# Gating a feed-forward layer in token halves, handed out one pair of slices later

## The chip, the cores and the metric

The kernel is one program on one core of a Trainium2 chip. The metric is the device time of one execution in microseconds (us); lower is better. Everything is 32-bit floating point.

## What is computed

Eight sequences of 128 tokens with 512 features go through one cross-attention layer and one gated feed-forward layer. The reference, cut to its frame and to the part that the change touches:

```python
x = x + xattn(layernorm(x), ctx, mask, position_bias, ...)      # 32 heads of 128
# feed-forward: Wg, Wu are (1376, 512), Wd is (512, 1376)
h    = layernorm(x)
gate = einsum('bsh,ih->bsi', h, Wg) * ag
up   = einsum('bsh,ih->bsi', h, Wu) * au
out  = einsum('bsi,hi->bsh', silu(gate) * up, Wd) * ad
x    = x + out
```

`silu(g)` is `g * sigmoid(g)`. The step `silu(gate) * up` is called the gating below.

## The kernel before

The kernel runs in stages: keys, values and queries; attention by groups of four heads; the output projection; and the feed-forward layer, which takes the last fifth of the time. Only the last stage matters here.

All 1024 tokens lie along the free dimension, in two halves of 512[...]. The 1376 inner features are cut into ten slices of 128 and one of 96. The slice of 96 is worked out apart (`last_slice`). The ten others go in five pairs, `i` from 0 to 4. In each pair a Strassen-like scheme (`seven`) replaces eight block products by seven, for the gate weights (`t = 0`) and the up weights (`t = 1`) in turn: fourteen products, counted by `n` from 0 to 13. A product is two `nc.tensor.matmul` calls (L688), which the profile shows as four MATMULs. After each product its PSUM bank is added into or copied to two tiles in SBUF. For `n` = 0 and 1 that is a copy on ScalarE (L235), for 2 and 3 an addition on VectorE (L240), for 4 to 9 copies on ScalarE (L245), and for 10 to 13 additions on VectorE (L251). The gate's result goes to the tiles `gate[0]` and `gate[1]`, one for each slice of the pair; the up result goes straight to `act[2*i]` and `act[2*i+1]`.

The banks tie TensorE to the other engines. Products 4 to 9 use the two banks of products 2 and 3 again, so product 4 cannot start until the addition of product 2 (L240) has read its bank. In the same way 12 and 13 reuse the banks of 10 and 11. Each pair takes fresh banks for products 0, 2 and 10 from a ring of seven.

After the fourteenth product of a pair, `gated` is called for each of its two slices. It issues a sigmoid on ScalarE (L639) into a tile `sg`, then `sg = gate * ag * sg` (L640) and `act = act * au * sg` (L643) on VectorE, each over all 1024 tokens. VectorE runs its queue in order, so what is queued there first delays what follows.

GpSimd (POOL) forms the weight sums for the coming pairs (`sums_a`, L193 to L196: four additions for the gate weights, four for the up weights). The sums of pair `i + 2` go into buffers that pair `i` gives back with its last products, so they run just as pair `i` ends. The weights themselves are loaded by the SP queue (L617).

`gate`, `sg`, and several tiles that live to the end of the stage come from one pool, `acts`, of 18 equal buffers: four of `x1`, four of `h2`, four of token sums `T1` to `T4`, and the rest for `gate` and `sg`. When all pairs are done, the loop over `b` multiplies with the down weights: eleven products for each sequence (L712, `ic` 10 first and then 0 to 9), a scaling and the residual addition on VectorE (L716, L717), and the store (L718).

The instructions stand in the engines' queues in the order that a scheduling step gives them. It follows the program where it can, but lets an instruction that is ready go ahead of one that is not.

Of the kernel before, what the change touches and what calls it, by code (L numbers as in the profile page):

```python
# [2 lines left out]

# [13 lines left out]
P = 128  # L17
# [8 lines left out]
def xattn_ffn_kernel(  # L26
# [164 lines left out]
    def sums_a(eng, a11, a12, a21, a22, s1, s2, s4):  # L191

        eng.tensor_tensor(s1, a21, a22, ADD)  # L193
        eng.tensor_tensor(s2, s1, a11, SUB)
        eng.tensor_tensor(a21, a11, a21, SUB)
        eng.tensor_tensor(s4, a12, s2, SUB)  # L196
        return {1: a11, 2: a12, 3: s4, 4: a22, 5: s1, 6: s2, 7: a21}
# [26 lines left out]
    def seven(name, tiles, product, part, pool, tag="mm"):  # L224


        def bank(i):
            return [
                pool.tile([P, 512], F32, tag=tag, name=f"mm_{name}_{i}_{t}") for t in tiles
            ]  # L230

        m = bank(2)
        for t in tiles:
            product(2, t, m[t], True)
            nc.scalar.copy(part(1, 1, t), m[t])  # L235
            yield
        m = bank(1)
        for t in tiles:
            product(1, t, m[t], True)
            nc.vector.tensor_tensor(part(1, 1, t), part(1, 1, t), m[t], ADD)  # L240
            yield
        for i, r, c in ((6, 1, 2), (7, 2, 2), (4, 2, 1)):
            for t in tiles:
                product(i, t, m[t], False)
                nc.scalar.copy(part(r, c, t), m[t])  # L245
                yield
        m = bank(5)
        for i, r, c in ((5, 2, 2), (3, 1, 2)):
            for t in tiles:
                product(i, t, m[t], i == 5)  # L250
                nc.vector.tensor_tensor(part(r, c, t), part(r, c, t), m[t], ADD)  # L251
                yield
# [359 lines left out]
    def load_gate_up(i, eng=nc.sync):  # L612
        c0, n = i * 2 * P, min(2 * P, INTER - i * 2 * P)
        tiles = []
        for nm, src in (("wg", wgT), ("wu", wuT)):
            t = fw.tile([P, DC, 2 * P], F32, tag="w", name=f"{nm}_{i}")
            eng.dma_start(  # L617
                t[:, :, :n], src[:, c0 : c0 + n].rearrange("(c p) n -> p c n", p=P)
            )
            tiles.append(t)  # L620
        return tiles

    def load_down():
        t = wdp.tile([P, NI, D], F32, tag="wd", name="wd")
        full = INTER // P
        nc.sync.dma_start(t[:, :full, :], wdT[: full * P, :].rearrange("(c p) n -> p c n", p=P))
        if INTER % P:
            nc.sync.dma_start(t[: INTER % P, full, :], wdT[full * P :, :])
        return t

    act = [actp.tile([P, T], F32, tag="act", name=f"act_{ic}") for ic in range(NI)]
# [5 lines left out]
    def gated(act, gate, up, ic, m, sg):  # L637

        nc.scalar.activation(sg, gate, AF.Sigmoid, scale=ag_sb[:m, ic : ic + 1])  # L639
        nc.vector.scalar_tensor_tensor(  # L640
            sg, gate, ag_sb[:m, ic : ic + 1], sg, ALU.mult, ALU.mult
        )
        nc.vector.scalar_tensor_tensor(  # L643
            act, up, au_sb[:m, ic : ic + 1], sg, ALU.mult, ALU.mult
        )

    def last_slice(th):

        ic, m = NI - 1, INTER - (NI - 1) * P
        o = []  # L650
        for w, nm in zip(alone, ("gp", "up")):
            o.append(ps.tile([P, 512], F32, tag="m", name=f"{nm}_{th}"))
            for c in range(DC):
                nc.tensor.matmul(  # L654
                    o[-1][:m], w[:, c, :m], h2[c // HC, th][:, c % HC, :],
                    start=(c == 0), stop=(c == DC - 1),
                )
        sg = work.tile([P, 512], F32, tag="pT", name=f"sg_{th}", bufs=4)
        gated(act[ic][:m, bass.ts(th, 512)], o[0][:m], o[1][:m], ic, m, sg[:m])
# [10 lines left out]
    nc.vector.tensor_tensor(t4, h2[1, 0], t2, SUB)  # L670
    h2_t = {1: h2[0, 0], 2: h2[1, 0], 3: h2[1, 1], 4: t4, 5: t1, 6: t2, 7: t3}

    for i in range(NP):
        ws, gate = [], [acts.tile([P, T], F32, tag="a", name=f"gate_{i}_{r}") for r in range(2)]
        for nm, w in zip("gu", gate_up[i]):
            s = fw.tile([P, 3, HC, P], F32, tag="S", name=f"S_{nm}{i}")
            ws.append(sums_a(
                nc.gpsimd, w[:, :HC, :P], w[:, HC:, :P], w[:, :HC, P:], w[:, HC:, P:],
                s[:, 0], s[:, 1], s[:, 2],
            ))  # L680
        if i + 1 < NP:
            gate_up.append(load_gate_up(i + 1))
        if i == 0:
            wd = load_down()

        def product(n, t, out, first):
            for c in range(HC):
                nc.tensor.matmul(  # L688
                    out, ws[t][n][:, c, :], h2_t[n][:, c, :],
                    start=(first and c == 0), stop=(c == HC - 1), skip_group_check=True,  # L690
                )

        def part(r, c, t):
            return (gate[r - 1], act[2 * i + r - 1])[t][:, bass.ts(c - 1, 512)]

        for n, _ in enumerate(seven(f"f{i}", range(2), product, part, ps, "m")):
            if i == 0 and n == 3:
                last_slice(1)
        for r in range(2):
            ic = 2 * i + r  # L700
            sg = acts.tile([P, T], F32, tag="a", name=f"sg_{ic}")
            gated(act[ic], gate[r], act[ic], ic, P, sg)

    for b in range(B):
        r = work.tile([P, D], F32, tag="aT", name=f"r_{b}")
        parts = 1 if b + 1 < B else 2
        for k in range(parts):
            cols = bass.ts(k, D // parts)
# [53 lines left out]
```

## Time and profile before

| what | value |
|---|---|
| median of 3 runs | 1152.94 us (1151.9 to 1153.74) |
| the profiled execution: its own time | 1155.07 us |
| the profiled execution: span from first to last instruction | 1153.3 us |
| TensorE (PE) busy | 1116.4 us, 97% |
| VectorE (DVE) busy | 501.0 us, 43% |
| ScalarE (ACT) busy | 317.4 us, 28% |
| GpSimd (POOL) busy | 307.3 us, 27% |
| share of the chain that ended last: PE, DVE | 90%, 4% |
| mean granted TensorE clock | 0.992 of full speed |

The span runs from the first instruction to the last; the time of the profiled execution is 1.77 us longer, which lies around it. It is one execution, 2.13 us above the median. "Busy" counts the instructions' own durations; PEld is the loading of weights into TensorE. The chain that ended last is followed back from the last instruction, at each step to what released it; only work on that chain sets the time.

### The profile page before, as it was taken

The page shows a single profiled execution, that of the slowest core. Times are in us where ns is not written, and L with a number is a line of the kernel's source. Part 1 is how long each engine was busy: PE and PEld are TensorE (multiplying, and loading weights), DVE is VectorE, ACT ScalarE, POOL GpSimd, SP SyncE. Part 2 cuts the span into 40 slices and gives each one's busy share as a digit, 9 for nine tenths or more (in the row PEclk, how much of TensorE's full clock was granted, in tenths as well). Part 3 has the DMA queues.
Part 4 walks back from the last instruction along what each step waited for, and adds up shares of the span by engine and source line. Part 5 has one row for each costly group of instructions (what it writes and reads, how often), then busy time and mean ns, then how long its engine had stood idle before and what let it go on. Part 6 is the DMA issues. An engine that isn't in the chain of part 4 may idle for free.

```text
span 1153.3 us, 12296 instructions
## 1 busy us (share of the span) xinstructions
PE 1116.4 (97%) x4286; PEld 729.4 (63%) x4286; DVE 501.0 (43%) x937; ACT 317.4 (28%) x889; POOL 307.3 (27%) x255
## 2 busy tenths in 40 slices
PE   6899999999999999999999999689999999999998
PEld 3564444445867677686858688578888864444445
DVE  4541111116555556555555557724433253433311
ACT  2521112223444344434344433301000022222000
POOL 5331221116333333333223314530000034330000
PEclk9999999999999999999999999899999999999999
DMA  9114423257646465555554446864222322110000
GB/s 281 43 37 149 178 110 110 109 204 252 187 138 200 145 192 162 176 181 174 184 172 148 135 146 199 256 217 170 92 92 80 116 99 73 36 37 1 15 31 28
DMA packets 117534, 154.38 MB, mean 134 GB/s; under 512 B 12033, under 2 KB 71681, under 8 KB 117473
## 3 DMA queue, kind: packets, MB, share of 16 engines
q1 hardware_dynamic: 114784, 149.93, 40.4%
q10 hardware_dynamic: 2192, 2.10, 0.6%
q0 software_dynamic: 496, 1.58, 0.4%
q8 instruction: 34, 0.56, 0.2%
q14 instruction: 28, 0.22, 0.1%
HBM read 101.14 MB, written 52.43 MB: 133 GB/s over the span
## 4 chain that ended last, share of the span: by engine, by line
PE 90%; DVE 4%; DMA 4%; issue 1%; ACT 1%; SPq 0%; ACTq 0%; DVEq 0%
PE mm_q L261 17%; PE mm_v L279 16%; PE mm_k L261 15%; PE m L469 15%; PE mm_f L688 9%; PE dn L712 7%; PE sc L301 4%; PE av L357 4%; DMA turned<-tt 1%; DMA wk<-in_wkT_dram 1%; DVE sg L640 1%; DMA a<-att 1%; DVE act L643 1%; PE tp L152 1%; PE up L654 1%
## 5 line engine op out<-in xcount | busy, mean ns | idle before, releaser
L296 POOL TENSOR_TENSOR s<-pb,mneg 128x512 f32<-128x512 f32 x64 | 81.2, 1269 | 290.7 <-DVE tt L334 234.0
L261 PE MATMUL mm_k<-ctx_sb,wk 128*128 128x512 f32 x256 | 117.4, 603 | 7.5 <-DMA wk<-in_wkT_dram 4.4
L279 PE MATMUL mm_v<-wv,ctx_sb 128*128 128x256 f32 x512 | 115.9, 379 | 1.3 <-DMA wv<-in_wvT_dram 1.3
L261 PE MATMUL mm_q<-hT,wq 128*128 128x512 f32 x256 | 112.5, 592 | 0.0
L469 PE MATMUL m<-wo,a 128*128 128x256 f32 x400 | 100.6, 389 | 9.6 <-DMA a<-att 9.1
L311 ACT ACTIVATE s<-s,nmx 128x128 f32<-128x128 f32 x256 | 99.5, 390 | 37.4 <-DVE nmx L308 37.4
L279 PEld LDWEIGHTS mm_v<-wv,ctx_sb 128*128 128x128 f32 x512 | 95.1, 190 | 14.8 <-DMA wv<-in_wvT_dram 2.1
L362 ACT COPY aT<-av 128x512 f32<-128x512 f32 x64 | 37.5, 586 | 202.9 <-PE av L357 98.5
L261 PE MATMUL mm_k<-ctx_sb,S_k 128*128 128x512 f32 x192 | 87.8, 605 | 4.4 <-DVE k L240 4.0
L469 PEld LDWEIGHTS m<-wo,a 128*128 128x128 f32 x400 | 77.1, 196 | 21.2 <-DMA a<-att 9.5
L261 PEld LDWEIGHTS mm_q<-hT,wq 128*128 128x128 f32 x256 | 48.6, 190 | 60.8 <-issue 60.7
L279 PE MATMUL mm_v<-S_v,ctx_sb 128*128 128x256 f32 x384 | 86.4, 381 | 0.0
L261 PEld LDWEIGHTS mm_k<-ctx_sb,wk 128*128 128x128 f32 x256 | 46.9, 193 | 60.4 <-issue 45.2
L261 PE MATMUL mm_q<-hT,S_q 128*128 128x512 f32 x192 | 85.0, 592 | 0.0
L304 DVE TENSOR_TENSOR s<-sc,s 128x512 f32<-128x512 f32 x64 | 44.2, 690 | 86.0 <-PE sc L301 82.9
L301 PEld LDWEIGHTS sc<-k,q 128*128 128x128 f32 x512 | 67.4, 194 | 17.9 <-issue 13.4
L279 PEld LDWEIGHTS mm_v<-S_v,ctx_sb 128*128 128x128 f32 x384 | 71.7, 190 | 10.6 <-DVE v L251 1.5
L712 PE MATMUL dn<-wd,act 128*128 128x512 f32 (+3 forms) x198 | 75.8, 545 | 0.0
L251 DVE TENSOR_TENSOR q<-q,mm_q 128x512 f32<-128x512 f32 x32 | 22.0, 688 | 114.8 <-PE mm_q L261 114.8
L301 PE MATMUL sc<-k,q 128*128 128x128 f32 x512 | 68.1, 277 | 2.8 <-DMA q<-queries 2.8
L357 PE MATMUL av<-pT,v 128*128 128x128 f32 x512 | 67.9, 277 | 0.0
L261 PEld LDWEIGHTS mm_k<-ctx_sb,S_k 128*128 128x128 f32 x192 | 35.6, 193 | 48.6 <-issue 35.7
(156 smaller groups left out, 1494.3 us busy)
## 6 DMA issues: line engine op xcount, KB each, us to landing
queries<-q SPq DMA_DIRECT2D x32, 512.0 KB, 3.8
q<-queries SPq DMA_DIRECT2D x32, 512.0 KB, 4.5
turned<-tt SPq DMA_DIRECT2D x64, 256.0 KB, 2.2
pT<-turned SPq DMA_DIRECT2D x256, 64.0 KB, 2.5
att<-aT SPq DMA_DIRECT2D x64, 256.0 KB, 2.3
a<-att SPq DMA_DIRECT2D x32, 512.0 KB, 3.4
wq<-in_wqT_dram SPq DMA_DIRECT2D x8, 1024.0 KB, 5.6
wk<-in_wkT_dram SPq DMA_DIRECT2D x7, 1024.0 KB, 6.2
```

Source lines behind the costliest of these rows:

```text
L251: nc.vector.tensor_tensor(part(r, c, t), part(r, c, t), m[t], ADD)
L261: nc.tensor.matmul(out, w[i][:, c, bass.ts(t, P)], src[i][:, c, :], start=(first and c == 0), stop=(c == HC - 1), skip_group_check=True,)
L279: nc.tensor.matmul(out[:, bass.ts(k, HW)], src[i][:, c, bass.ts(2 * t + k, S)], w[i][:, c, :], start=(first and k == 0 and c == 0), stop=( ...
L296: nc.gpsimd.tensor_tensor(s, pb, mneg[:, b : b + 1, :].to_broadcast([P, GH, S]), ALU.add)
L301: nc.tensor.matmul(sc[:, j, :], qT[:, j, bass.ts(b % 2, S)], kT[j][:, cols], start=True, stop=True)
L304: nc.vector.tensor_tensor(s, sc, s, ALU.add)
L311: nc.scalar.activation(s[:, j, :], s[:, j, :], AF.Exp, bias=nmx[:, j : j + 1], accum_out=sm[:, j : j + 1],)
L357: nc.tensor.matmul(av[:, j, :], v[b // 2][:, b % 2, bass.ts(j, P)], pT[:, :, j, :], start=True, stop=True,)
L362: nc.scalar.copy(aT, av)
L469: nc.tensor.matmul(m[n], sa[n][:, c, :], wo_t[g][n][:, c, :], start=(g == order[0] and c == 0 and k % 2 == 0), stop=(g == order[-1] and c ...
L688: nc.tensor.matmul(out, ws[t][n][:, c, :], h2_t[n][:, c, :], start=(first and c == 0), stop=(c == HC - 1), skip_group_check=True,)
L712: nc.tensor.matmul(o, act[ic][:m, bass.ts(b, S)], wd[:m, ic, cols], start=(n == 0), stop=(n == NI - 1),)
```

## The change

The gating is no longer issued whole after the pair. Each slice's gating is cut into two pieces of 512 tokens, and the four pieces of a pair are put on a list. During the next pair's fourteen products one piece is taken from the list after each of the products `n` = 4, 6, 8 and 10, behind that product's own copy or addition. The list is in the order slice 0 first half, slice 0 second half, slice 1 first half, slice 1 second half. So sixteen of the twenty pieces are issued inside a following pair, and the last pair's four after the loop, ahead of the down products. The arithmetic is the same.

```diff
+    gatings = []
     for i in range(NP):
...
         for n, _ in enumerate(seven(f"f{i}", range(2), product, part, ps, "m")):
             if i == 0 and n == 3:
                 last_slice(1)
+            if 4 <= n < 12 and n % 2 == 0 and gatings:
+                gatings.pop(0)()
         for r in range(2):
             ic = 2 * i + r
             sg = acts.tile([P, T], F32, tag="a", name=f"sg_{ic}")
-            gated(act[ic], gate[r], act[ic], ic, P, sg)
+            for cols in (bass.ts(0, 512), bass.ts(1, 512)):
+                gatings.append(partial(
+                    gated, act[ic][:, cols], gate[r][:, cols], act[ic][:, cols], ic, P, sg[:, cols]
+                ))
+    for gating in gatings:
+        gating()
```

More of the change, by code (lines that the diff above doesn't have):

```diff
@@ L2 @@
 from contextlib import ExitStack
+from functools import partial
 import concourse.bass as bass
```

## The prediction

> **What bounds the kernel now.** I read the page's busy shares first, then the feed-forward stage alone (940 us to the end): who waited for whom, the chain that ended last, and the timelines of DVE, ACT and POOL around the end of each pair.
>
> ```profile
> PE 1116.4 (97%) x4286; PEld 729.4 (63%) x4286; DVE 501.0 (43%) x937; ACT 317.4 (28%) x889; POOL 307.3 (27%) x255
> ```
>
> TensorE is busy all but 37 us, so a change in this stage can only win where TensorE stands still. In the stage's list of waits TensorE's matmuls have one entry, three waits for L240, the addition that frees product 2's bank:
>
> ```profile
> PE mm_f L688 <- DVE gate L240: 3.7, 3, 1.2
> ```
>
> The chain that ended last shows the first of them (columns: start us, duration us, what):
>
> ```profile
> 973.40 0.69 DVE act L251
> 974.09 3.29 DVE sg L640 x2
> 977.38 1.19 DVE act L643
> 978.58 0.40 issue
> 978.98 1.31 DVE act L643
> 980.29 0.35 issue
> 980.64 0.69 DVE gate L240
> 981.33 0.14 issue
> 981.46 17.42 PE mm_f L688 x40
> ```
>
> Pair 0's last addition, its four gating instructions and only then L240 of pair 1 stand in DVE's queue. The same nine steps follow at 998.91 and 1024.41. Beside them POOL forms sums, and DVE's gating is slow:
>
> ```profile
> 974.00 3.38 DVE L640 SCALAR_TENSOR_TENSOR sg<-gate,ag_sb,sg 128x1024 f32<-128x1024 f32 x2
> 977.31 3.41 DVE L643 SCALAR_TENSOR_TENSOR act<-act,au_sb,sg 128x1024 f32<-128x1024 f32 x2
> ```
>
> At the fourth end of a pair POOL has nothing left to do. There the two rows of two last 2.47 us each, L240 comes in time and TensorE does not stop. The table by stretch shows it (five stretches of 10 us; the fifth is the last pair's gating under the down products):
>
> ```profile
> 972.00:982.00 10.00, 8.77 (x22) 3.66 (x21) 8.88 (x8) 3.36 (x4) 9.15 (x8) 1.00 0.00 0
> 997.50:1007.50 10.00, 8.77 (x22) 3.66 (x21) 8.89 (x8) 3.36 (x4) 9.15 (x8) 1.00 0.00 0
> 1023.00:1033.00 10.00, 8.77 (x22) 3.67 (x21) 8.89 (x8) 3.36 (x4) 9.15 (x8) 1.00 0.00 0
> 1048.50:1058.50 10.00, 10.00 (x25) 4.48 (x24) 7.13 (x8) 3.37 (x5) 0.00 (x0) 1.00 0.00 0
> 1072.50:1082.50 10.00, 10.00 (x25) 4.49 (x24) 5.88 (x6) 2.19 (x2) 0.00 (x0) 1.00 0.00 0
> ```
>
> The first figure after the length is PE's busy time: 8.77 of 10 at three ends, 10.00 at the fourth. By start times the loss is larger, because the ends of matmuls are modelled: products start 1.715 us apart, but product 4 starts 981.46 - 978.35 = 3.11 us after product 3. That is **1.40 us lost at each of three ends, 4.2 us in all**, the most this change can win by its mechanism.
>
> **What the skill says.** The Trainium skill, "SBUF — State Buffer", section "Who interferes with whom": a VectorE instruction with two SBUF inputs contends with a GpSimd instruction that reads SBUF; one with at most one SBUF input, outside the two-port modes, does not. The trace agrees: L640 and L643 take 1.71 us beside POOL and 1.28 without, POOL's sums 1.71 and 0.73, while L251, with one PSUM input, stays at 0.69. The page calls it an exclusive lock; measured, DVE took 6.64 us from 974.00 to L240 against 4.78 without POOL (1050.52 to 1055.30), and four POOL instructions ran meanwhile, so I use (6.64 - 4.78) / 4 = 0.47 us for each POOL instruction met. "Perfetto Trace Analysis", section "Optimizing Scalar/DVE Operations": "If Scalar/Vector aren't saturated, but are causing bubbles on other engines, breaking up instructions may allow work to be completed sooner." The bubble is there; no run here shows yet whether breaking up helps.
>
> **The change, part by part.** *Halves.* A sigmoid of 128x1024 takes 1142 ns; the nearest row of 128x512 with one per-partition operand is L175, 720 ns (bounds 683, the slice of 96, and 808, L596 with two operands). A half L640 or L643 is nearest to the slice of 96: 748 ns, 529 less than the 1277 of the whole. Queued back to back, whole ones came 4.78 / 4 = 1.195 us apart, so halves come 0.665 apart. Per pair ACT gets 4 x 0.72 - 2 x 1.14 = 0.6 us more and DVE 8 x 0.665 - 4.78 = 0.5 us more. Neither counts: in a pair of 24 us DVE idles 11.9 us ahead of product 10's addition and ACT idles 1.13 us after each copy. What covers them is this idle time; without it the whole would cost 5 x 0.5.
>
> *The move.* If the pieces stay where the program writes them, L240 follows the previous pair's last addition at once. Product 2 ends at 978.35, L240 starts 0.27 later and takes 0.69, and TensorE needs it by 978.35 + 1.715 = 980.06: 0.6 us to spare, all three stalls gone, **-4.2 us**. Later pieces hit idle engines. The tightest is the fourth, behind product 10's addition: that addition ends at 992.98, two halves at 994.31, product 11's addition follows, and TensorE can go on 0.82 us after its start (the distance from L240's start, 980.64, to 981.46) at 995.13; product 13 is due at 995.50. What is queued behind a piece on ACT is the next product's copy, ready 1.715 us after the one before; 0.59 + 0.72 fits.
>
> *Where the queue puts them.* The trace says the queue is not the program's order: `gated` issues L640, L643, L640, L643, yet both L640 run first, since the second was ready when the first L643 was not. A piece's inputs are ready long before product 4. One thing holds it back: in the trace the second slice's sigmoid, whose gate was whole at 969.0 (product 10's addition), did not run before the first's at 972.41, so a tile of `acts` seems not to be begun ahead of one begun earlier in the program. The first piece then has to follow the next pair's first copy (gate tile, 975.12), but needn't wait for product 4. The second piece shares its `sg` tile and follows at once; the third waits for product 6's copy, which begins the next gate tile. So I expect slice 0's two pieces just behind the first copy: sigmoid from 975.7 to 976.4, four halves on DVE from 976.42, done at 979.08 undisturbed, TensorE ready at 979.90, in time. POOL disturbs it: its third and fourth sum of the up weights, 0.69 apart from 974.59, now run at 975.97 and 976.66 and end near 977.4; one or two meet the halves. That adds 0.47 to 0.93: L240 at 979.55 to 980.01, TensorE at 980.37 to 980.83, a stall of 0.31 to 0.77 where 1.40 was. I take 0.4, near one meeting, since two meetings need both sums to be late. **3 x (1.40 - 0.4) = 3.0 us won.** The fourth end keeps 0.16 us to spare.
>
> *The end.* The last pair's eight halves come behind its last addition, 1074.6 + 8 x 0.665 = 1079.9. The first sequence's last down product, the tenth behind 1073.74 at 0.857 each, is due at 1082.3: covered. If it weren't, each 0.1 us late would cost 0.1 us.
>
> *Queues not touched.* No DMA is moved. SP's weight loads wait for products and POOL's sums for products 12 and 13 as before; POOL gets freer. The store queue is the same. Buffers: at the tightest moment `acts` holds 12 lasting tiles, two old gates, two `sg` and two new gates: 18, exactly what there is.
>
> **Sum.** 1155.07 - 3.0 = 1152.1 for the profiled execution. The median before stands 2.13 us lower, so 1152.94 - 3.0 = **1149.9**.
>
> **Rivals.** (1) *The pieces stay behind products 4 to 10:* all 4.2 us won, 1148.7. For it: the program says so. Against it: the reordered L640. 30%. (2) *The bunch ahead of L240 stays long:* all pieces slip ahead, or POOL's lock delays each half as it did each whole; four halves at 0.665 + 0.47 end at 980.96, TensorE at 981.8, 1.7 us late, or 5 us of halves as before. Then 1152 to 1154, no change within noise. Against it: POOL is through by 977.4, and the third piece waits for a gate tile. 15%. (3) *Slower: a nineteenth tile in* `acts`. If one more tile is held when product 6's copy begins the second gate tile, the copy waits until an old gate is given back, in the worst case with the fourth piece: two sigmoids and four halves behind product 6, 985.4 + 1.4 + 2.7 = 989.5, copy and release to 990.2, where product 8 was due at 986.92. That stalls 3.3 us in each of four pairs: 1152.94 + 13.2 - 4.2 = 1162. It decides from 1.05 us a pair. Against it: the count gives 18 and not 19. 5%, and 3% for a slowdown I don't see. My own case has 47%.
>
> **How the numbers follow.** Anything under 1150.6 is faster by over 0.2%, about what a measurement of this kernel can tell from no change. My case spans 3 x 0.63 = 1.9 to 4.2 us won, 1148.7 to 1151.0, and mostly counts as faster; with rival 1 that gives 76% faster. Its slow edge and rival 2 give 16% the same; 8% slower. The range takes in both likely cases, the low edge of rival 2, and the runs' scatter of about 0.8 us: 1148.0 to 1151.9.
>
> **What would show it.** Twice as many L639, L640 and L643 of 128x512 near 720 and 745 ns. In the waits, TensorE's 3.7 us for L240 shrinks below 2 or vanishes; in the stretches around the first three ends PE rises above 9.3. In DVE's timeline four halves stand before L240 (mine) or none (rival 1). The feed-forward stage's POOL sums of the up weights fall from 1.71 us towards 0.73. A wait of ACT's copies on DVE would be rival 3. Three stalls of over 1 us left, or new waits at products 6 to 13, would prove me wrong.

## The result, and the profile after

The changed kernel takes 1151.96 us in the median of 20 runs, against 1153.88 us for the kernel before in the same series. The ratio of the two series is 0.998, with a 95% interval of 0.9974 to 0.9986. That is 2.3 us less (1.6 to 3.0), two thousandths; the two medians by themselves lie 1.9 apart. The prediction forecast 3.0 us less, and so 1149.9 with a range of 1148.0 to 1151.9, from the three runs then shown, whose median was 1152.94. The measured median lies 0.06 above that range, but in the longer series the kernel before is 0.94 higher too: 2.3 us off 1152.94 would be 1150.6. The profiled execution took 1152.01 us, span 1150.2 us, against 1155.07 and 1153.3.

The line of the page with each engine's busy time (share of the span, instructions) shows the added instructions, 20 on DVE and 10 on ACT, and 9.4 us less on POOL, whose sums are lengthened less by VectorE. PE's busy time, which contains modelled ends, differs by several us among the profiles of all kernels here and is not read:

```profile
PE 1120.0 (97%) x4286; PEld 731.4 (64%) x4286; DVE 502.3 (44%) x957; ACT 318.1 (28%) x899; POOL 297.9 (26%) x255
```

In the waits of the feed-forward stage (us in total, times, longest) the one entry of TensorE's matmuls is still there, and smaller. L240 of the kernel before is L241 here:

```profile
PE mm_f L690 <- DVE gate L241: 1.0, 3, 0.3
```

The chain that ended last, at the first end of a pair (start us, duration us, what), answers to the nine steps shown of before:

```profile
974.77 0.02 ACT gate L236
974.80 0.46 issue
975.26 0.73 ACT sg L640
975.99 0.03 issue
976.01 2.13 DVE sg L641 x2
978.14 1.32 DVE act L644 x2
979.47 0.61 DVE gate L241
980.08 0.14 issue
980.22 19.14 PE mm_f L690 x44
```

The gating of slice 0, now four half instructions, still stands ahead of the addition that TensorE needs. It no longer starts at the pair's last addition but behind the next pair's first copy, and it is four halves where four wholes had been. TensorE's rows for products 3 and 4 there:

```profile
978.01 1.88 PE L690 MATMUL mm_f<-h,wu 128*128 128x512 f32 x4
980.22 1.96 PE L690 MATMUL mm_f<-T_h,S_g 128*128 128x512 f32 x4 [0.33 <-DVE gate L241]
```

Product 3 began at 978.01, so product 4 was due 1.715 us later, at 979.73; it began at 980.22. **0.49 us are lost at each of three ends, where it had been 1.40.** The table by stretch (10 us around each end; the first figure after the length is PE's busy time) says the same, with the fourth end again undisturbed:

```profile
971.70:981.70 10.00, 9.67 (x24) 4.09 (x23) 5.68 (x8) 2.30 (x4) 5.74 (x8) 1.00 0.00 0
996.50:1006.50 10.00, 9.67 (x23) 4.10 (x22) 5.43 (x8) 2.29 (x4) 5.54 (x8) 1.00 0.00 0
1021.10:1031.10 10.00, 9.68 (x23) 4.10 (x22) 5.48 (x8) 2.30 (x4) 5.53 (x8) 1.00 0.00 0
1045.50:1055.50 10.00, 10.00 (x25) 4.42 (x24) 5.02 (x8) 2.37 (x5) 0.00 (x0) 1.00 0.00 0
```

Whole-kernel times scatter by several us between runs, and so does the time at which this stage begins. A sharper measure is the stage itself in a profile: from the first matmul of `last_slice` (into `gp`) to the first down product (into `dn`). These rows hold the two times, first of the kernel before, then of the changed one:

```profile
L654 PE MATMUL gp<-h,wg x16: 592/592/592, 934.6 to 952.2; 128*96 128x512 f32 x16
L712 PE MATMUL dn<-wd,act x198: 377/592/594, 1073.7 to 1149.1; 128*128 128x512 f32 x140, 128*128 128x256 f32 x40, 96*128 96x512 f32 x14, 96*128 96x256 f32 x4
L655 PE MATMUL gp<-h,wg x16: 592/592/592, 934.2 to 951.8; 128*96 128x512 f32 x16
L721 PE MATMUL dn<-wd,act x198: 377/592/594, 1070.7 to 1146.1; 128*128 128x512 f32 x140, 128*128 128x256 f32 x40, 96*128 96x512 f32 x14, 96*128 96x256 f32 x4
```

With the two decimals of the timelines that is 1073.74 - 934.55 = 139.19 us before and 1070.68 - 934.21 = 136.47 after. The stage is 2.7 us shorter, which is the three stalls, 3 x (1.40 - 0.49) = 2.7.

### The profile page after: what moved, and what is told of

The parts are those of the page before. It is cut to its first block, busy times and chain, and to the rows that moved or that the text cites. A ratio compares the mean times of both kernels' runs of the same rounds, so it can differ in the third digit from the quotient of the medians.

```text
span 1150.2 us, 12321 instructions
## 1 busy us (share of the span) xinstructions
PE 1120.0 (97%) x4286; PEld 731.4 (64%) x4286; DVE 502.3 (44%) x957; ACT 318.1 (28%) x899; POOL 297.9 (26%) x255
## 4 chain that ended last, share of the span: by engine, by line
PE 91%; DVE 4%; DMA 2%; ACT 1%; issue 1%; POOL 0%; SPq 0%; ACTq 0%; DVEq 0%
PE mm_q L262 17%; PE mm_v L280 16%; PE m L470 16%; PE mm_k L262 16%; PE mm_f L690 9%; PE dn L721 7%; PE sc L302 4%; PE av L358 4%; DMA wk<-in_wkT_dram 1%; DMA wo<-in_woT_dram 1%; PE tp L153 1%; PE up L655 1%; PE gp L655 1%; DVE sg L641 1%; ACT s L312 0%
## 5 line engine op out<-in xcount | busy, mean ns | idle before, releaser
L252 DVE TENSOR_TENSOR q<-q,mm_q 128x512 f32<-128x512 f32 x32 | 22.0, 688 | 114.8 <-PE mm_q L262 114.8
```

## The experiments

My theory: TensorE's loss is set by what stands in VectorE's queue ahead of product 2's addition and by POOL's sums that run beside it; the changed kernel leaves four halves of the one and parts of the last two sums of the other. The rivals: that handing the pieces out is what gains, or that halving is, or that what is left comes with the list itself. The stage is read from one profile of each kernel. The table collects all kernels; the text after it takes them one by one.

| kernel | ratio to before (95% interval) | stage, us | waits of TensorE for product 2's addition |
|---|---|---|---|
| before | 1 | 139.2 | 3.7 us, 3 times |
| changed | 0.998 (0.9974 to 0.9986) | 136.5 | 1.0 us, 3 times |
| whole slices, handed out | 0.9987 (0.9976 to 0.9998) | 136.9 | 1.2 us, 3 times |
| halves, not handed out | 0.9962 (0.9954 to 0.9971) | 134.8 | none |
| handed out from product 6 on | 0.9966 (0.9955 to 0.9976) | 134.8 | none |
| before, six sum buffers | 0.9969 (0.9957 to 0.9981) | 134.8 | none |
| changed, six sum buffers | 0.9967 (0.9956 to 0.9978) | 134.8 | none |
| changed, `sg` in its own buffers | 0.9975 (0.9961 to 0.9989) | 134.8 | none |
| changed, three tiles more held | one run only | 136.5 | 1.0 us, 3 times |

### The move alone

```diff
-            for cols in (bass.ts(0, 512), bass.ts(1, 512)):
+            for cols in (slice(0, T),):
```

> The move alone: each slice's gating stays one piece of 1024 tokens and is taken from the list behind products 4 and 6 of the next pair. If what counts is what stands in VectorE's queue ahead of product 2's addition (L241), the first slice's whole gating slips ahead of it as the two halves did: sigmoid 1.14 us from the first copy, two instructions 1.195 us apart and one meeting with a POOL sum at 0.47, so L241 comes about 0.3 us later than in an undisturbed row and three stalls of 0 to 0.5 us are left; 2.7 to 4.2 us less than before, ratio 0.9965 to 0.998. If the halving is what made the gain, the stalls stay near 1.4 us and the ratio near 1.

The ratio is 0.9987, and the stage 2.3 us shorter than before. Two wholes instead of four stand ahead of L241. The timelines of VectorE, POOL and TensorE at the first end:

```profile
977.59 1.79 DVE L641 SCALAR_TENSOR_TENSOR sg<-gate,ag_sb,sg 128x1024 f32<-128x1024 f32 x1 [2.70 <-ACT sg L640]
979.42 1.28 DVE L644 SCALAR_TENSOR_TENSOR act<-act,au_sb,sg 128x1024 f32<-128x1024 f32 x1
980.62 0.68 DVE L241 TENSOR_TENSOR gate<-gate,mm_f 128x512 f32<-128x512 f32 x1
```

```profile
977.57 0.74 POOL L197 TENSOR_TENSOR S_u<-wu,S_u 128x256 f32<-128x256 f32 x1
```

```profile
979.16 1.88 PE L690 MATMUL mm_f<-h,wu 128*128 128x512 f32 x4
981.45 1.96 PE L690 MATMUL mm_f<-T_h,S_g 128*128 128x512 f32 x4 [0.41 <-DVE gate L241]
```

TensorE went on at 981.45 where product 4 was due at 980.88 (product 3 at 979.16): 0.57 us lost. Stall and ratio both lie a little beyond what was expected (0.5 us and 0.998), but nowhere near 1.4 us. So the halving is not what made most of the gain; moving half of the work away from the end of the pair did. The move does two things at once: fewer instructions stand ahead of L241, and they start later, when most of POOL's sums are over. This kernel does not part the two. The one POOL sum that began 0.02 us ahead of L641 cost it 1.79 - 1.28 = 0.51 us and was itself not slowed. The same page of the Trainium skill that the prediction names ("SBUF — State Buffer", "Who interferes with whom") says "Issue order, not op shape, decides who blocks", and this is such a case.

### The halving alone

```diff
-            if 4 <= n < 12 and n % 2 == 0 and gatings:
+            if False and gatings:
                 gatings.pop(0)()
...
                     gated, act[ic][:, cols], gate[r][:, cols], act[ic][:, cols], ic, P, sg[:, cols]
                 ))
-    for gating in gatings:
-        gating()
+        while gatings:
+            gatings.pop(0)()
```

> The halving alone: the four pieces are issued straight behind the pair, no list. If the handing out made the gain, the eight half instructions stand ahead of the next pair's L241 and the stalls are as long as before or 0.3 us longer: ratio 1 to 1.001. If only what is in the queue ahead of L241 counts, three of the four pieces are ready before the pair ends (each half of a slice is complete as soon as its own products are in) and go between the pair's own copies and additions; only the second half of the first slice is left, two instructions done by 975.5 us against L241's 978.6: no stall at all, 4.2 us less than before, ratio 0.9964, and 1.5 us less than the changed kernel.

The ratio is 0.9962, TensorE has no wait for the addition, and the stage is 4.4 us shorter than before, 1.7 us shorter than with the change. VectorE's timeline of pair 0, from the first piece on to the next pair's first addition, shows why:

```profile
965.80 0.97 DVE L641 SCALAR_TENSOR_TENSOR sg<-gate,ag_sb,sg 128x512 f32<-128x512 f32 x1 [5.64 <-ACT sg L640]
966.82 0.75 DVE L644 SCALAR_TENSOR_TENSOR act<-act,au_sb,sg 128x512 f32<-128x512 f32 x1
969.37 0.75 DVE L641 SCALAR_TENSOR_TENSOR sg<-gate,ag_sb,sg 128x512 f32<-128x512 f32 x1 [1.81 <-ACT sg L640]
970.33 0.75 DVE L644 SCALAR_TENSOR_TENSOR act<-act,au_sb,sg 128x512 f32<-128x512 f32 x1 [0.21 <-ACT act L246]
971.43 0.69 DVE L252 TENSOR_TENSOR gate<-gate,mm_f 128x512 f32<-128x512 f32 x1 [0.35 <-PE mm_f L690]
972.91 0.75 DVE L641 SCALAR_TENSOR_TENSOR sg<-gate,ag_sb,sg 128x512 f32<-128x512 f32 x1 [0.79 <-ACT sg L640]
973.58 0.68 DVE L252 TENSOR_TENSOR act<-act,mm_f 128x512 f32<-128x512 f32 x1
974.30 0.75 DVE L644 SCALAR_TENSOR_TENSOR act<-act,au_sb,sg 128x512 f32<-128x512 f32 x1
974.97 0.68 DVE L252 TENSOR_TENSOR gate<-gate,mm_f 128x512 f32<-128x512 f32 x1
976.44 1.24 DVE L641 SCALAR_TENSOR_TENSOR sg<-gate,ag_sb,sg 128x512 f32<-128x512 f32 x1 [0.79 <-ACT sg L640]
977.60 0.67 DVE L252 TENSOR_TENSOR act<-act,mm_f 128x512 f32<-128x512 f32 x1
978.31 1.19 DVE L644 SCALAR_TENSOR_TENSOR act<-act,au_sb,sg 128x512 f32<-128x512 f32 x1
981.80 0.69 DVE L241 TENSOR_TENSOR gate<-gate,mm_f 128x512 f32<-128x512 f32 x1 [2.30 <-PE mm_f L690]
```

Three of the four pieces run among the pair's own copies and additions, in idle time that the prediction had counted (11.9 us) but only the next pair was to use. By the program, slice 0 as a whole is complete only with the additions of products 12 and 13 and slice 1 with those of 10 and 11; the first half of slice 0 is complete with product 3, that of slice 1 with product 9. The last piece meets POOL's sums (1.24 and 1.19 us instead of 0.75), but VectorE then idles 2.30 us before L241. The handing out is therefore not what the gain needs; beside the halving it takes 1.7 us back.

### The pieces from product 6 on

```diff
-            if 4 <= n < 12 and n % 2 == 0 and gatings:
+            if 6 <= n < 10 and gatings:
```

> The changed kernel with the pieces taken behind products 6, 7, 8 and 9 in place of 4, 6, 8 and 10, so that no piece's sigmoid can begin before the next pair's second gate tile does at product 6. If the bunch ahead of L241 is the rest of the loss: nothing of the gating stands there, no wait of TensorE for L241, 1.5 us less than the changed kernel, 4.2 less than before, ratio 0.9964. The eight halves then take 5.3 us from product 6's copy on and are through 0.5 us before product 10's addition. If the rest is something else (a wait that comes with the list itself), the time stays that of the changed kernel, 0.998.

The ratio is 0.9966, no wait is left, and the stage is 134.8 us. In VectorE's timeline L241 follows the last L252 with 4.53 us of idle time between them, and the eight halves come from 988.12 on, behind product 6's copy:

```profile
980.08 0.69 DVE L241 TENSOR_TENSOR gate<-gate,mm_f 128x512 f32<-128x512 f32 x1 [4.53 <-PE mm_f L690]
988.12 1.41 DVE L641 SCALAR_TENSOR_TENSOR sg<-gate,ag_sb,sg 128x512 f32<-128x512 f32 x2 [5.63 <-ACT sg L640]
```

There they meet no sum of POOL, and each pair of halves takes 1.41 us. What the changed kernel still loses thus comes from the bunch ahead of L241, and the list as such costs nothing.

### POOL's sums out of the way: before and changed

```diff
-            s = fw.tile([P, 3, HC, P], F32, tag="S", name=f"S_{nm}{i}")
+            s = fw.tile([P, 3, HC, P], F32, tag="S", name=f"S_{nm}{i}", bufs=6)
```

On the kernel before:

> The kernel before with six buffers in place of four for POOL's weight sums, nothing else, so that the sums of a coming pair needn't wait for the pair's end and run some 3 us after its weights are loaded, in mid-pair. If POOL's sums beside the gating are what made the three stalls, every pair's end looks like the fourth one of before: the four gating instructions 1.195 us apart, L240 0.46 us ahead of its due time, no stall, 4.2 us less, ratio 0.9964. If the gating's place in the queue is enough by itself, the stalls stay 1.4 us and the ratio 1.

The ratio is 0.9969 and the waits are gone, with the gating still whole and still where it had been. POOL's sums now run from 969.20 to 974.95 and only the last of them meets the gating:

```profile
974.22 0.73 POOL L196 TENSOR_TENSOR S_u<-wu,S_u 128x256 f32<-128x256 f32 x1
974.53 2.71 DVE L640 SCALAR_TENSOR_TENSOR sg<-gate,ag_sb,sg 128x1024 f32<-128x1024 f32 x2
977.16 2.47 DVE L643 SCALAR_TENSOR_TENSOR act<-act,au_sb,sg 128x1024 f32<-128x1024 f32 x2
979.55 0.68 DVE L240 TENSOR_TENSOR gate<-gate,mm_f 128x512 f32<-128x512 f32 x1
```

One number changes in the program, the order of the instructions on TensorE, VectorE, ScalarE and GpSimd stays the same through the pairs, none is split, and the whole 4.4 us come: the stalls of the kernel before came from POOL's sums running beside VectorE's gating. On the changed kernel:

> The changed kernel with six buffers in place of four for POOL's weight sums, nothing else; the order of the queues is the changed kernel's, with four halves ahead of L241. If POOL's sums beside the halves are all that is left of the stall, L641 takes 0.74 us everywhere (0.85 in the mean now), four halves take 2.66 us as at the fourth end of the changed kernel, L241 comes about 0.2 us ahead of its due time and TensorE never waits for it: 1.5 us less than the changed kernel, ratio 0.9965. If the queue's order alone left the stall, three waits of 0.5 us stay and the ratio is 0.998.

The ratio is 0.9967. The four halves ahead of L241 stay where they were, now undisturbed, and TensorE does not wait (the two L641 take 1.42 us where they took 2.13; product 4 began at 978.90, as it was due):

```profile
975.19 1.42 DVE L641 SCALAR_TENSOR_TENSOR sg<-gate,ag_sb,sg 128x512 f32<-128x512 f32 x2 [2.27 <-ACT sg L640]
976.52 1.41 DVE L644 SCALAR_TENSOR_TENSOR act<-act,au_sb,sg 128x512 f32<-128x512 f32 x2
977.85 0.68 DVE L241 TENSOR_TENSOR gate<-gate,mm_f 128x512 f32<-128x512 f32 x1
978.90 1.88 PE L690 MATMUL mm_f<-T_h,S_g 128*128 128x512 f32 x4
```

So either cause can be taken away, and each is enough: without POOL the bunch fits, and without the bunch POOL does no harm.

### What holds a piece back

```diff
-            sg = acts.tile([P, T], F32, tag="a", name=f"sg_{ic}")
+            sg = actp.tile([P, T], F32, tag="sg", name=f"sg_{ic}", bufs=2)
```

> The changed kernel with the sg tiles in two buffers of their own, in place of the pool acts; pieces, list and the products behind which they are taken are unchanged. If it is the order in which tiles of acts are begun that holds a piece back until the next pair's first copy, the first half of each slice now runs inside its own pair, only the second half of slice 0 is left for the pair's end, and the stalls are gone: ratio 0.9965. One half then stands between the two additions of L241, where it has 0.6 us to spare. If something else holds the pieces back, four halves stay ahead of L241, three stalls of 0.5 us, ratio 0.998.

The ratio is 0.9975, with an interval that holds both 0.9965 and 0.998, so the time alone decides nothing. The profile does: no wait for the addition, stage 134.8 us, and the first half of slice 1 runs inside its own pair, at 966.11, where VectorE had idled:

```profile
966.11 0.75 DVE L641 SCALAR_TENSOR_TENSOR sg<-gate,ag_sb,sg 128x512 f32<-128x512 f32 x1 [9.21 <-ACT sg L640]
```

That `sg` came from `acts` is thus what held the changed kernel's pieces back. It was not a shortage of buffers there, as the next kernel shows; the order in which tiles of one pool are begun fits all timelines here, from which it is inferred.

### Three tiles more in the pool

```diff
     gatings = []
+    held = [acts.tile([P, T], F32, tag="a", name=f"held_{k}") for k in range(3)]
+    for t in held:
+        nc.vector.memset(t[:, :1], 0.0)
...
+    for k, t in enumerate(held):
+        u = small.tile([P, 1], F32, tag="ss", name=f"seen_{k}")
+        nc.vector.tensor_tensor(u, t[:, :1], act[2 * NP - 1][:, T - 1 :], ADD)
```

> The changed kernel with three more tiles of acts taken before the pairs (three tiny VectorE writes of 128x1) and read only behind the last piece (three tiny additions), so that three buffers fewer are left to gate and sg. The third rival of the prediction said one tile more stalls product 8 by 3.3 us in each of four pairs. As slice 0's pieces run before product 2's addition, its gate and sg are given back long before product 6 begins the second gate tile, and one of the h2 tiles is free after the first pair: 11 lasting tiles, two old gates, one new, one sg, 15 at the most. Then three more change nothing: three waits of TensorE for L241 as in the changed kernel, none at product 8. If the rival is right, waits of 3 us at product 8 appear.

In its profile the stage takes 136.5 us and TensorE waits 1.0 us in three waits for L241, as in the changed kernel; none appears at product 8. The whole time, 1149.4 us, is a single run and is not read further.

## Why the prediction was right, and where it was off

**The limit of 4.2 us.** It came from the start times of products, not from the idle time that the waits show (3.7 us). Five kernels reach it and a little more: 139.2 - 134.8 = 4.4 us. The prediction counted only the delay of product 4; after a stall, product 5 too starts 1.80 us behind it (981.46 to 983.26) instead of 1.715, which makes 3 x (1.40 + 0.08) = 4.4.

**The halves.** A half sigmoid was put at 720 ns and measures 717. A half L641 or L644 was put at 748 ns and measures 744 to 750 where POOL is quiet. Four in a row were put at 2.66 us; at the fourth end they took 1052.46 - 1049.80 = 2.66.

**The place in the queue.** This was the step that decided between 3.0 and 4.2 us, and it held: copy, two sigmoids, four halves, then L241. The first half began 1.24 us after the first copy did (976.01 - 974.77), and 1.30 had been worked out. The reason given, the order in which tiles of `acts` are begun, is borne out by the kernel with its own `sg` buffers. Rival 1, the program's order, falls; so does rival 2, since three quarters of an us of contention were met and not four times 0.47.

**The contention.** Here the range held (0.47 to 0.93 us of contention, a stall of 0.31 to 0.77) and the value taken from it was off: I leaned to one meeting, a stall of 0.4. Measured: the first two halves took 2.13 us instead of 1.41, so 0.72, and the stall is 0.49. The halves began at 976.01, while the third sum still ran, and met all of the fourth:

```profile
975.74 0.73 POOL L196 TENSOR_TENSOR wu<-wu 128x256 f32<-128x256 f32 x1
976.43 1.17 POOL L197 TENSOR_TENSOR S_u<-wu,S_u 128x256 f32<-128x256 f32 x1
```

The prediction's own times said so already: its third sum, from 975.97 for 0.73 us, ends at 976.70, after the first half begins at 976.42. That two meetings "need both sums to be late" does not follow from them. The stage won 0.09 us less at each of three ends: 2.7 us instead of 3.0. The price for each POOL instruction is no constant either: it was 0.51 for the wholes, from a sum that began just ahead, and 0.72 for the halves from the end of one sum and the whole of the next.

**The end.** The last pair's eight halves were to come behind its last addition, by 1079.9. That was wrong in a harmless way: with no later gate tile ahead of them, three of the four pieces ran among the pair's own products, and the last half ended at 1072.86. The down products did not wait, as forecast.

**Rival 3.** The count of 18 tiles was too high. Slice 0's `gate` and `sg` are given back before slice 1's `sg` begins, and one `h2` tile is free after the first pair; three more tiles changed nothing. There never was a danger at the nineteenth.

**What I had not asked.** The prediction priced halving as a cost and the move as the gain. It did not ask what halves could do without the move, though its own remark that a ready instruction goes ahead of one that is not leads there. The kernel with halves only does better than the change, with less code: ratio 0.9962 (0.9954 to 0.9971), below the whole interval of the changed kernel. It is not told apart from the other kernels whose stage takes 134.8 us. As no wait of TensorE for VectorE is left in the stage, none of the variants can gain more by this path.

## What to carry to other kernels

Where an instruction order follows readiness, cutting an operation to the size in which its inputs come in lets it start in the pair's own idle time; postponing it by hand can put it in a worse place. Before moving work off a busy queue, look at what runs beside it: here one buffer count, which sets when another engine's work becomes ready, gave the whole gain. And judge a change of two thousandths by the stage's own length in a profile of each kernel, which separated 136.5 from 134.8 us where the intervals of the whole times partly overlap.

## What the runs showed of the hardware

A GpSimd sum of 128x256 beside VectorE's gating did not always cost the same. In the kernel with whole slices handed out, a sum that began 0.02 us ahead of VectorE's instruction kept its 0.74 us, and VectorE lost 0.51. In the changed kernel, where VectorE's was running first, the sum grew from 0.73 to 1.17 us. The exclusive lock that the page describes, held for the whole instruction, would have cost VectorE 0.72 us in the first case, the time that the sum still had to run. Measured it was less, and no run here shows why.
